# A second in-place fold in the bias network: eight key pairs to a packed tile, half the third-layer matmuls

## The chip, the cores and the metric

The kernel runs on one core of a Trainium2 chip. Its engines are TensorE (PE; its weight loads are shown as PEld), VectorE (DVE), ScalarE (ACT), GpSimd (POOL) and SyncE (SP); POOL and SP issue the DMAs of the stage that is changed here. The metric is the device time of one execution in microseconds. Three runs of the kernel before took 2696.52, 2698.0 and 2698.18 us, so their median is 2698.0 us.

## The reference

Four layers are computed one after the other on an image tensor; only the first matters here. It is a deformable attention block on x of shape (2, 512, 32, 32), with 8 heads of 64 channels. For every image and head, 64 key positions are found from the queries by an offset network, the input is sampled there, and keys and values are made from the samples. A small network of three layers gives a bias for every pair of one of the 1024 query pixels and one of the 64 keys:

```python
pos = grid_q[:, :, None, :] - grid_kv[:, None, :, :]
bias = jnp.sign(pos) * jnp.log1p(jnp.abs(pos))
bias = jax.nn.relu(bias @ cpb_w1 + cpb_b1)
bias = jax.nn.relu(bias @ cpb_w2 + cpb_b2)
bias = (bias @ cpb_w3 + cpb_b3).reshape(b, GROUPS, H * W, Hd * Wd)
sim = jnp.einsum('bhid,bhjd->bhij', qh, kh) + bias
attn = jax.nn.softmax(sim, axis=-1)
out = jnp.einsum('bhij,bhjd->bhid', attn, vh)
```

The hidden layers have 128 units. An output projection and an MLP follow in the same block, then the three other layers. All data is fp32.

## The kernel before

Two heads share a chunk of 128 channels, so there are 8 groups g (four chunks k, two images b) with 64 keys j, each key standing for both heads. One long loop goes through all 512 keys as 256 pairs p. A step number n counts keys; pair p covers n = 2p and 2p+1.

**First layer.** `first(n)` (L346, one custom VectorE instruction at L353) adds a table of column terms and one of row terms and clips at zero: a tile `h1` of 128 units by 2048 (pixels of both heads). Four such tiles exist (L343). The tables are loaded by SyncE (`tab_load`, L157) and scaled by ScalarE.

**Second layer.** `second(p, o)` (L612) runs for o = 0 to 3, each for 32 of the 128 hidden units. Eight matmuls (L619) write 32 output rows each, four of them side by side in the 128 rows of a `ph` tile (rows 32t to 32t+31 hold the quarter t of head and pixels), for the two keys of the pair. ScalarE applies bias and relu while copying to the tile `r0` to `r3` (L628); two `ph` tiles alternate.

**Third layer.** Its weights are not applied in one matmul over 128 units. Hidden units are ordered and scaled at the start of the kernel (`counted`, L462) so that units that are added unweighted share a weight's sign. `combine` (L631, VectorE, at L634) adds `r1` times a ratio to `r0`, and `r3` likewise to `r2`. `join` (L636, L637) adds `r2` to `r0` by an accumulating DMA from POOL's queue. `fold` (L639, L642) adds the odd rows of `r0` to the even rows, in place, by another one. `shift` (L644, a plain DMA by SyncE at L649) copies every fourth row of `r0` into a packed tile `xs`, and `meet` (L651, L653, POOL) adds the rows two further to them, so that a row of `xs` holds the sum of four neighbouring rows. Four pairs share an `xs` tile. `third` (L655, matmuls at L664) contracts packed tiles with the sparse weights `cw3` into `psim`: each call has four matmuls of 32 rows, and two calls accumulate into one `psim` tile, so that a group takes four calls, 16 matmuls.

**Order of the work.** Inside the loop all instructions of an engine keep the order in which the program issues them (`pin`). `at(n, when, fn)` puts work on a date; `run(n, when)` issues it at step n after an even o (when = 0) or an odd o (when = 1). Pair p is folded at step 2p+4, shifted at 2p+6 and met at 2p+7 (L909 to L911); the join of a pair is issued in the next pair after o = 1 (L942). Third-layer calls of a group stand at 64g + 16u + 24. `prepare` (L674) samples and projects keys and values of a group, from step 64(g-1) + 32 on; in it `keys` (L735, ScalarE) and `values` (L741, VectorE) copy into `kblk` and `vblk` in four pieces each. `weigh` (L747) and `weights` (L759) multiply values with the output weights into `vwo`, one slot for each of the 8 groups. `attend` (L780) does the softmax of a group, from step 64(g+1) + 9 on. `chain` (L913) computes the key positions of later groups; its 36 taps per call (L230, VectorE) are spread over steps 4 to 86 and 97 to 213. `r0` has five buffers, `xs` three.

After the loop the remaining folds, shifts and meets run, then the last third-layer call and the last softmax. Here the order is not pinned: the compiler's scheduler mixes in the output projection `po` (L1040, 64 matmuls, of which 32 belong to image 0). The `po` matmuls take `vwo` as weights. The MLP follows (L1105).

Of the kernel before, what the change touches and what calls it, by code (L numbers as in the profile page):

```python
# [10 lines left out]
F32 = mybir.dt.float32  # L11
AF = mybir.ActivationFunctionType
ALU = mybir.AluOpType
# [3 lines left out]
P = 128  # L17
B, C, H, W = 2, 512, 32, 32
# [39 lines left out]

_ORDER = [("same", P), ("below", P), ("place", P), ("rank", 1), ("third", 33)]
_CAT, _n = {}, 0  # L60
# [12 lines left out]
def conv_seq(  # L73
# [61 lines left out]
    with ExitStack() as ctx_l0:  # L135
# [11 lines left out]

        vwo = l0.tile([P, KC * B, C], F32, name="vwo")
        nc.gpsimd.memset(kblk, 0.0)
# [37 lines left out]
        def pin(ins):  # L187
            return tc.keep_in_program_order(ins) if started else ins
# [150 lines left out]
        sb3 = l0.tile([P, 4, 2], F32, name="sb3")  # L339
        cw3 = l0.tile([P, 33], F32, name="cw3")  # L340
        rel = l0.tile([P, 2], F32, name="rel")
# [23 lines left out]
        with tc.tile_pool(name="a", bufs=1) as a, tc.tile_pool(name="aps", bufs=3, space=PSUM) as aps, tc.tile_pool(  # L365
# [96 lines left out]
            def counted():  # L462
                pin(ve.tensor_copy(od[:, 7:9], pcnt))
                pin(ve.tensor_scalar(cpbw, cpbw, maj, None, ALU.mult))


                pin(ve.tensor_scalar(maj, total, 8.0, None, ALU.is_ge))
                pin(ve.tensor_scalar(t0, maj, -1.0, 1.0, ALU.mult, ALU.add))
                pin(ve.tensor_scalar(t1, total, -1.0, 16.0, ALU.mult, ALU.add))
# [125 lines left out]


        with tc.tile_pool(name="hid", bufs=3) as hid, tc.tile_pool(name="sm", bufs=1) as sm, tc.tile_pool(name="hps", bufs=2, space=PSUM) as hps, tc.tile_pool(
            name="sps", bufs=1, space=PSUM
# [13 lines left out]
            def second(p, o):  # L612

                ph = hps.tile([P, 2, 512], F32, name="ph")
                for i in range(2):
                    for t in range(4):
# [9 lines left out]
                        )  # L626
                r = hid.tile([P, 2, 512], F32, name=f"r{o}", bufs=(5, 1, 3, 1)[o])
                pin(nc.scalar.activation(r, ph, AF.Relu, bias=sb3[:, o, 1:2]))  # L628
# [9 lines left out]

            def fold(p):  # L639

                r = rs[p, 0]
                pin(nc.gpsimd.dma_start(r[0::2], r[1::2], accum_op=ALU.add))  # L642

            def shift(p):  # L644

                t, d = divmod(p, 4)
                if d == 0:
                    xs_[t] = hid.tile([P, 2, 512], F32, name="xs", bufs=3)
                pin(nc.sync.dma_start(xs_[t][d::4], rs[p, 0][0::4]))  # L649

            def meet(p):  # L651
                t, d = divmod(p, 4)
                pin(nc.gpsimd.dma_start(xs_[t][d::4], rs.pop((p, 0))[2::4], accum_op=ALU.add))  # L653

            def third(g, u):  # L655
                kb, i = divmod(u, 2)
                if i == 0:
                    psims[g, kb] = sps.tile([P, 512], F32, name=f"psim{kb}")
                for a in range(2):
                    xs = xs_.pop(g * J // 8 + 2 * u + a)  # L660
                    for c in range(2):
                        m = 2 * c + a
                        pin(
                            nc.tensor.matmul(  # L664
                                psims[g, kb][m * 32 : (m + 1) * 32, :],
                                lhsT=cw3[:, 1 - i : 33 - i],
                                rhs=xs[:, c, :],
                                start=(i == 0),
                                stop=(i == 1),
                                skip_group_check=True,  # L670
                            )
                        )

            def prepare(g):  # L674

                k, b = divmod(g, B)
                st = {}
                n = J * (g - 1) + 32
                here = slice(CO_AT[k] * P + b * J, CO_AT[k] * P + (b + 1) * J)
# [50 lines left out]
                def ordered(to, of):  # L730

                    to, of = to.rearrange("p (c x i) -> p c x i", c=2, i=2), of.rearrange("p (i x c) -> p c x i", c=2, i=2)
                    return to, of

                def keys():  # L735
                    for h, kb in np.ndindex(2, 2):
                        hs, ks = slice(h * DH, (h + 1) * DH), slice(kb * 32, (kb + 1) * 32)
                        to, of = ordered(kblk[hs, g % 2, h, ks], st["pk"][hs, 0, ks])
                        pin(nc.scalar.activation(to, of, AF.Identity, scale=DH**-0.5))

                def values():  # L741
                    for h, kb in np.ndindex(2, 2):
                        hs, ks = slice(h * DH, (h + 1) * DH), slice(kb * 32, (kb + 1) * 32)
                        to, of = ordered(vblk[hs, g % 2, h, ks], st["pk"][hs, 1, ks])
                        pin(nc.vector.tensor_copy(to, of))
# [13 lines left out]
                def weights():  # L759
                    pin(nc.scalar.copy(vwo[:, g, :], st["pw"]))  # L760

# [140 lines left out]
            for g in range(NG):  # L902
                prepare(g)
                for u in range(4):
                    at(J * g + 16 * u + 24, 0, third, g, u)
                if g < NG - 1:
                    attend(g, J * (g + 1) + 9, True)
            for p in range(NK // 2):
                at(2 * p + 4, 0, fold, p)  # L909
                at(2 * p + 6, 0, shift, p)  # L910
                at(2 * p + 7, 0, meet, p)  # L911

# [15 lines left out]

            chain(1, 2, 86, 82)
            chain(2, 4, 213, 116)  # L930

# [103 lines left out]
        for t in range(NT // 512):  # L1035
            ts_ = slice(t * 512, (t + 1) * 512)
            for o in range(KC):
                po = mh.tile([P, 512], F32, name="po")
                for k in range(KC):
                    nc.tensor.matmul(  # L1040
                        po,
                        lhsT=vwo[:, k * B + t // 2, o * P : (o + 1) * P],
                        rhs=q[:, k, ts_],
                        start=(k == 0),
                        stop=(k == KC - 1),
                    )
# [838 lines left out]
def _layout(a):  # L1885
# [50 lines left out]

    rank = p // 32 * 4 + p % 4
    same = p[:, None] % 32 // 4 == p[None] % 32 // 4
    put("same", same.astype(f), order)
    put("below", (same & (rank[:, None] < rank[None])).astype(f), order)  # L1940
    put("place", (np.array([0, 2, 1, 3])[p // 32] * 4 + p % 4).astype(f)[None], order)
    put("rank", rank.astype(f)[:, None], order)

    put("third", (np.arange(33)[None] == (1 + 8 * (p // 32) + 2 * (p % 4))[:, None]).astype(f), order)
    put("npy", -(4 * np.arange(8)[None] + p[:, None] // 32).astype(f))
# [56 lines left out]
```

## Time and profile before

| what | value |
|---|---|
| median of three runs | 2698.0 us |
| the profiled execution, own time | 2697.67 us |
| its span on the page | 2695.9 us, granted TensorE clock 0.996 |
| PE busy | 2653.6 us, 98% |
| VectorE busy | 2251.3 us, 84% |
| ScalarE busy | 1538.4 us, 57% |
| POOL busy | 669.8 us, 25% |
| second layer, L619 | 16384 matmul records, 1779.1 us |
| first layer, L353 | 512 instructions, 1172.9 us, 2291 ns each |
| `combine`, L634 | 512 instructions, 658.0 us, 1285 ns each |
| evictions, L628 | 1024 instructions, 1141.1 us, 1114 ns each |
| POOL's issues of join, fold, meet | 958, 857, 1198 ns each, 256 of each |

An fp32 matmul appears in the profile as two records. Busy shares are means over the whole program; the loop of the bias network fills 34 to 1901 us of it. An engine's idle time is listed with what ended it. For a DMA the page gives the time from its issue to its landing, and the issuing engine counts only the issue as busy.

### The profile page before, as it was taken

What the parts mean: (1) busy time and instruction counts of PE and PEld (TensorE: products, weight loads), DVE (VectorE), ACT (ScalarE), POOL (GpSimd) and SP (SyncE); (2) the same over time, 40 slices, a digit from 0 to 9 for tenths busy, and PEclk for the clock granted to TensorE, in tenths of its full rate; (3) what the DMA queues carried; (4) which work ended last, traced back from release to release, by engine and by line L of the source; (5) the groups of instructions that cost most, each with busy time, mean ns of one, the idle gap of its engine ahead of it and who ended that gap; (6) DMA issues with size and microseconds to landing.
All of it is one profiled execution on the core that took longest, in us unless ns stands there. A gap on an engine that the chain in (4) does not pass through costs nothing.

```text
span 2695.9 us, 48423 instructions
## 1 busy us (share of the span) xinstructions
PE 2653.6 (98%) x19574; PEld 967.3 (36%) x19574; DVE 2251.3 (84%) x2009; ACT 1538.4 (57%) x1920; POOL 669.8 (25%) x784
## 2 busy tenths in 40 slices
PE   8999999999999999999999999999999999999997
PEld 4223323232332323333333333333444444455544
DVE  6999999999999999999999999999554445525646
ACT  7676677777667777866877776776221111001334
POOL 0333333333333333333333333333100000000001
PEclk9999999999999999999999999999999999999998
DMA  4777877877777787787788788787400000100001
GB/s 129 165 165 162 168 158 161 169 157 162 163 166 158 165 170 157 165 168 161 162 195 173 154 179 188 163 174 159 94 30 24 16 24 24 62 17 1 1 0 63
DMA packets 109327, 335.04 MB, mean 124 GB/s; under 512 B 18576, under 2 KB 28304, under 8 KB 108336
## 3 DMA queue, kind: packets, MB, share of 16 engines
q0 software_dynamic: 69632, 234.93, 46.7%
q1 hardware_dynamic: 38896, 96.51, 10.4%
q8 instruction: 154, 2.52, 0.4%
q14 instruction: 69, 0.57, 0.1%
q10 hardware_dynamic: 576, 0.51, 0.1%
HBM read 58.99 MB, written 4.46 MB: 24 GB/s over the span
## 4 chain that ended last, share of the span: by engine, by line
PE 81%; DVE 9%; issue 6%; ACT 2%; DMA 1%; POOL 1%; DVEq 0%; ACTq 0%; POOLq 0%
PE ph L619 51%; DVE h L353 4%; PE A L1105 4%; PE D L1105 4%; PE C L1105 4%; DVE r L634 3%; PE B L1105 2%; PE po L1040 2%; PE pg L1248 1%; PE pa L1359 1%; PE pu L1282 1%; PE psim L664 1%; PE pscore L1491 1%; DMA xs<-r 1%; PE pt L1511 1%
## 5 line engine op out<-in xcount | busy, mean ns | idle before, releaser
L619 PE MATMUL ph<-h,w2a 128*32 128x512 f32 x16384 | 1779.1, 593 | 6.0 <-ACT r L628 3.3
L628 ACT ACTIVATE r<-ph,sb 128x1024 f32<-128x1024 f32 x1024 | 1141.1, 1114 | 510.5 <-PE ph L619 487.3
L353 DVE CUSTOM_DVE_ANT_1 h<-tab 128x2048 f32<-128x2048 f32 x512 | 1172.9, 2291 | 13.0 <-PE ph L619 10.0
L619 PEld LDWEIGHTS ph<-h,w2a 128*32 128x32 f32 x16384 | 520.2, 109 | 1226.6 <-issue 801.7
L634 DVE SCALAR_TENSOR_TENSOR r<-r,rel,r 128x1024 f32<-128x1024 f32 x512 | 658.0, 1285 | 16.4 <-ACT r L628 15.8
L642 POOL DMA_DIRECT2D r<-r x256 | 219.5, 857 | 961.2 <-DMA r<-r 936.1
L637 POOL DMA_DIRECT2D r<-r x256 | 245.2, 958 | 280.4 <-DVE r L634 243.6
L653 POOL DMA_DIRECT2D xs<-r x256 | 306.6, 1198 | 12.2 <-issue 6.1
L173 ACT ACTIVATE tab<-tab,vec 128x256 f32<-128x256 f32 x252 | 136.9, 543 | 0.0
L1293 POOL MEMSET M<- 128x512 f32 x2 | 1.0, 524 | 435.3 <-DVE x L1169 435.3
L1145 ACT COPY u<-A 128x512 f32<-128x512 f32 x16 | 9.4, 585 | 146.9 <-PE A L1105 146.9
L1776 POOL TENSOR_TENSOR x<-x,aff 128x512 f32<-128x512 f32 x7 | 7.0, 1031 | 329.0 <-ACT e L1741 329.0
L1124 ACT ACTIVATE h<-h,vec 128x512 f32<-128x512 f32 x32 | 23.1, 721 | 113.7 <-DVE h L1127 113.7
L1127 DVE TENSOR_TENSOR h<-C,u 128x512 f32<-128x512 f32 x32 | 22.1, 691 | 48.2 <-PE C L1105 47.9
L1105 PE MATMUL A<-xn,w 128*128 128x512 f32 x128 | 60.3, 593 | 0.8 <-DVE x L1047 0.8
L1105 PE MATMUL C<-hT,w 128*128 128x512 f32 x128 | 60.3, 592 | 0.0
L1105 PE MATMUL A<-h,w 128*128 128x512 f32 x128 | 60.1, 592 | 0.0
L1040 PE MATMUL po<-q,vwo 128*128 128x512 f32 x128 | 56.3, 594 | 0.0
L230 DVE SCALAR_TENSOR_TENSOR acc<-q,vec,acc 128x128 f32<-128x128 f32 (+3 forms) x88 | 46.2, 525 | 0.8
L1165 DVE TENSOR_TENSOR x<-D,x 128x512 f32<-128x512 f32 x32 | 22.1, 691 | 25.8 <-PE D L1105 25.7
L856 ACT ACTIVATE e<-e,den 128x64 f32<-128x64 f32 x128 | 41.8, 338 | 1.9 <-DVE den L852 1.9
L1165 DVE TENSOR_TENSOR x<-C,x 128x512 f32<-128x512 f32 x32 | 22.1, 690 | 24.8 <-PE C L1105 24.8
(365 smaller groups left out, 1867.6 us busy)
## 6 DMA issues: line engine op xcount, KB each, us to landing
r<-r POOLq DMA_DIRECT2D x256, 512.0 KB, 5.2
r<-r POOLq DMA_DIRECT2D x256, 256.0 KB, 3.4
xs<-r SPq DMA_DIRECT2D x256, 128.0 KB, 3.9
xs<-r POOLq DMA_DIRECT2D x256, 128.0 KB, 5.6
tab<-fd SPq DMA_DIRECT2D x63, 512.0 KB, 5.6
lw<-in_l_w_dram SPq DMA_DIRECT2D x5, 1024.0 KB, 9.0
x<-in_x_dram SPq DMA_DIRECT2D x4, 1024.0 KB, 10.5
w<-in_mlp_w_dram SPq DMA_DIRECT2D x8, 512.0 KB, 4.3
```

The lines of the kernel that those rows point to most:

```text
L173: return nc.scalar.activation(tf, tf if src is None else src[:, :, ax, :], AF.Identity, bias=0.0 if ax == 0 else v("L0_conv_cpb_b1"), scal ...
L230: pin(nc.vector.scalar_tensor_tensor(dst, src, wt_, dst, ALU.mult, ALU.add))
L353: nc.vector._custom_dve(TENSOR_ADD_SAT, out=h1, in0=columns.unsqueeze(1).to_broadcast([P, 32, 2, 32]), in1=rows_.unsqueeze(3).to_broadcast ...
L619: nc.tensor.matmul(ph[t * 32 : (t + 1) * 32, i, :], lhsT=w2a[:, o], rhs=h1s[2 * p + i][:, half * 16 : (half + 1) * 16, h, :], start=True, ...
L628: pin(nc.scalar.activation(r, ph, AF.Relu, bias=sb3[:, o, 1:2]))
L634: pin(nc.vector.scalar_tensor_tensor(r0, r1, rel[:, i : i + 1], r0, ALU.mult, ALU.add))
L637: pin(nc.gpsimd.dma_start(rs[p, 0], rs.pop((p, 2)), accum_op=ALU.add))
L642: pin(nc.gpsimd.dma_start(r[0::2], r[1::2], accum_op=ALU.add))
L653: pin(nc.gpsimd.dma_start(xs_[t][d::4], rs.pop((p, 0))[2::4], accum_op=ALU.add))
L1040: nc.tensor.matmul(po, lhsT=vwo[:, k * B + t // 2, o * P : (o + 1) * P], rhs=q[:, k, ts_], start=(k == 0), stop=(k == KC - 1),)
L1105: nc.tensor.matmul(banks[bank], lhsT=a[an][k], rhs=b_[bn_][k], start=(i < 4 and k == 0), stop=(k == n - 1), skip_group_check=True,)
L1165: nc.vector.tensor_tensor(to, t, to, ALU.add)
```

## The change

The packed sum is taken one step further by DMA. A second in-place fold adds rows that lie two apart (now sums of two) so that every fourth row of `r0` holds a sum of four; `shift` then copies every eighth row, and `meet` adds the rows four further. Eight pairs fill an `xs` tile, a row of it holds the sum of eight neighbouring rows, and a group takes two third-layer calls with four matmuls each, 8 in place of 16; nothing accumulates in `psim` between calls. The hidden units are ordered for classes of eight rows instead of four per quarter, `cw3` has 32 columns instead of 33, and the keys' order in `kblk` and `vblk` changes so that two copies do instead of four. `r0` gets a sixth buffer. `vwo` keeps only image 0; the weights of image 1 are written over `wo`, whose slice is not read any more. Some dates move by two steps.

```diff
-                r = hid.tile([P, 2, 512], F32, name=f"r{o}", bufs=(5, 1, 3, 1)[o])
+                r = hid.tile([P, 2, 512], F32, name=f"r{o}", bufs=(6, 1, 3, 1)[o])
...
-            def fold(p):
+            def fold(p, step):
                 r = rs[p, 0]
-                pin(nc.gpsimd.dma_start(r[0::2], r[1::2], accum_op=ALU.add))
+                pin(nc.gpsimd.dma_start(r[0 :: 2 * step], r[step :: 2 * step], accum_op=ALU.add))
             def shift(p):
-                t, d = divmod(p, 4)
+                t, d = divmod(p, 8)
                 if d == 0:
                     xs_[t] = hid.tile([P, 2, 512], F32, name="xs", bufs=3)
-                pin(nc.sync.dma_start(xs_[t][d::4], rs[p, 0][0::4]))
+                pin(nc.sync.dma_start(xs_[t][d::8], rs[p, 0][0::8]))
             def meet(p):
-                t, d = divmod(p, 4)
-                pin(nc.gpsimd.dma_start(xs_[t][d::4], rs.pop((p, 0))[2::4], accum_op=ALU.add))
-            def third(g, u):
-                kb, i = divmod(u, 2)
-                if i == 0:
-                    psims[g, kb] = sps.tile([P, 512], F32, name=f"psim{kb}")
+                t, d = divmod(p, 8)
+                pin(nc.gpsimd.dma_start(xs_[t][d::8], rs.pop((p, 0))[4::8], accum_op=ALU.add))
+            def third(g, kb):
+                psims[g, kb] = sps.tile([P, 512], F32, name=f"psim{kb}")
                 for a in range(2):
-                    xs = xs_.pop(g * J // 8 + 2 * u + a)
+                    xs = xs_.pop(g * J // 16 + 2 * kb + a)
...
-                                lhsT=cw3[:, 1 - i : 33 - i],
+                                lhsT=cw3,
                                 rhs=xs[:, c, :],
-                                start=(i == 0),
-                                stop=(i == 1),
+                                start=True,
+                                stop=True,
...
-                n = J * (g - 1) + 32
+                n = J * (g - 1) + 34
...
                 def values():
-                    for h, kb in np.ndindex(2, 2):
-                        hs, ks = slice(h * DH, (h + 1) * DH), slice(kb * 32, (kb + 1) * 32)
-                        to, of = ordered(vblk[hs, g % 2, h, ks], st["pk"][hs, 1, ks])
+                    for h in range(2):
+                        hs = slice(h * DH, (h + 1) * DH)
+                        to, of = ordered(vblk[hs, g % 2, h, :], st["pk"][hs, 1, :])
                         pin(nc.vector.tensor_copy(to, of))
...
-                    pin(nc.scalar.copy(vwo[:, g, :], st["pw"]))
+                    pin(nc.scalar.copy((vwo, wo)[b][:, k, :], st["pw"]))
...
-                for u in range(4):
-                    at(J * g + 16 * u + 24, 0, third, g, u)
+                for kb in range(2):
+                    at(J * g + 32 * kb + 42, 0, third, g, kb)
                 if g < NG - 1:
-                    attend(g, J * (g + 1) + 9, True)
+                    attend(g, J * (g + 1) + 11, True)
             for p in range(NK // 2):
-                at(2 * p + 4, 0, fold, p)
-                at(2 * p + 6, 0, shift, p)
-                at(2 * p + 7, 0, meet, p)
+                at(2 * p + 4, 0, fold, p, 1)
+                at(2 * p + 6, 0, fold, p, 2)
+                at(2 * p + 8, 0, shift, p)
+                at(2 * p + 9, 0, meet, p)
...
-            chain(1, 2, 86, 82)
-            chain(2, 4, 213, 116)
+            chain(1, 2, 88, 84)
+            chain(2, 4, 215, 116)
```

More of the change, by code (lines that the diff above doesn't have):

```diff
@@ L57 @@
 _CONSTS = [("ident", P), ("grid", 2 * J), ("gridf", J), ("npx", 1), ("npy", 8), ("sel3", 2)]
-_ORDER = [("same", P), ("below", P), ("place", P), ("rank", 1), ("third", 33)]
+_ORDER = [("same", P), ("below", P), ("place", P), ("rank", 1), ("third", 32)]
 _CAT, _n = {}, 0
@@ L146, in conv_seq @@
         smpp = ctx_att.enter_context(tc.tile_pool(name="smp", bufs=1))
-        vwo = l0.tile([P, KC * B, C], F32, name="vwo")
+        vwo = l0.tile([P, KC, C], F32, name="vwo")
         nc.gpsimd.memset(kblk, 0.0)
@@ L339, in conv_seq @@
         sb3 = l0.tile([P, 4, 2], F32, name="sb3")
-        cw3 = l0.tile([P, 33], F32, name="cw3")
+        cw3 = l0.tile([P, 32], F32, name="cw3")
         rel = l0.tile([P, 2], F32, name="rel")
@@ L464, in counted @@
                 pin(ve.tensor_scalar(cpbw, cpbw, maj, None, ALU.mult))
-                pin(ve.tensor_scalar(maj, total, 8.0, None, ALU.is_ge))
+                pin(ve.tensor_scalar(maj, total, 16.0, None, ALU.is_ge))
                 pin(ve.tensor_scalar(t0, maj, -1.0, 1.0, ALU.mult, ALU.add))
-                pin(ve.tensor_scalar(t1, total, -1.0, 16.0, ALU.mult, ALU.add))
+                pin(ve.tensor_scalar(t1, total, -1.0, 32.0, ALU.mult, ALU.add))
                 pin(ve.scalar_tensor_tensor(t0, t1, t0, below, ALU.mult, ALU.add))
@@ L730, in ordered @@
                 def ordered(to, of):
-                    to, of = to.rearrange("p (c x i) -> p c x i", c=2, i=2), of.rearrange("p (i x c) -> p c x i", c=2, i=2)
+                    to, of = to.rearrange("p (k c x) -> p k c x", k=2, c=2), of.rearrange("p (k x c) -> p k c x", k=2, c=2)
                     return to, of
                 def keys():
-                    for h, kb in np.ndindex(2, 2):
-                        hs, ks = slice(h * DH, (h + 1) * DH), slice(kb * 32, (kb + 1) * 32)
-                        to, of = ordered(kblk[hs, g % 2, h, ks], st["pk"][hs, 0, ks])
+                    for h in range(2):
+                        hs = slice(h * DH, (h + 1) * DH)
+                        to, of = ordered(kblk[hs, g % 2, h, :], st["pk"][hs, 0, :])
                         pin(nc.scalar.activation(to, of, AF.Identity, scale=DH**-0.5))
                 def values():
-                    for h, kb in np.ndindex(2, 2):
-                        hs, ks = slice(h * DH, (h + 1) * DH), slice(kb * 32, (kb + 1) * 32)
-                        to, of = ordered(vblk[hs, g % 2, h, ks], st["pk"][hs, 1, ks])
+                    for h in range(2):
+                        hs = slice(h * DH, (h + 1) * DH)
+                        to, of = ordered(vblk[hs, g % 2, h, :], st["pk"][hs, 1, :])
                         pin(nc.vector.tensor_copy(to, of))
@@ L1041, in conv_seq @@
                         po,
-                        lhsT=vwo[:, k * B + t // 2, o * P : (o + 1) * P],
+                        lhsT=(vwo, wo)[t // 2][:, k, o * P : (o + 1) * P],
                         rhs=q[:, k, ts_],
@@ L1934, in _layout @@
     put("sel3", (p[:, None] % 32 == np.array([1, 2])[None]).astype(f))
-    rank = p // 32 * 4 + p % 4
-    same = p[:, None] % 32 // 4 == p[None] % 32 // 4
+    rank = p // 32 * 8 + p % 8
+    same = p[:, None] % 32 // 8 == p[None] % 32 // 8
     put("same", same.astype(f), order)
     put("below", (same & (rank[:, None] < rank[None])).astype(f), order)
-    put("place", (np.array([0, 2, 1, 3])[p // 32] * 4 + p % 4).astype(f)[None], order)
+    put("place", (np.array([0, 2, 1, 3])[p // 32] * 8 + p % 8).astype(f)[None], order)
     put("rank", rank.astype(f)[:, None], order)
-    put("third", (np.arange(33)[None] == (1 + 8 * (p // 32) + 2 * (p % 4))[:, None]).astype(f), order)
+    put("third", (np.arange(32)[None] == (8 * (p // 32) + p % 8)[:, None]).astype(f), order)
     put("npy", -(4 * np.arange(8)[None] + p[:, None] // 32).astype(f))
```

## The prediction

> **What bounds the kernel now.** The bias network's loop runs from 34 to 1901 us. I cut it into windows first, then asked the waits of its two halves, then the timeline around one third-layer call, the groups, the DMA landings and the chain. Windows (columns: window, busy us and instruction count of PE, PEld, DVE, ACT, POOL, then clock, DMA share, GB/s):
>
> ```profile
> 400.00:600.00 200.00, 199.65 (x1863) 62.10 (x1859) 199.23 (x139) 145.20 (x171) 69.41 (x81) 1.00 0.79 163
> 1400.00:1600.00 200.00, 200.00 (x1854) 61.95 (x1846) 194.26 (x124) 146.48 (x178) 72.47 (x84) 1.00 0.80 169
> ```
>
> TensorE looks full in both, but a busy PE is modelled. VectorE tells them apart: 199.2 of 200 us early, 194.3 late. The waits of 100 to 860 us, then of 880 to 1850 us (us in total, times, longest):
>
> ```profile
> PEld ph L619 <- DVE h L353: 30.4, 45, 1.3
> DVE h L353 <- PE ph L619: 0.4, 1, 0.4
> ...
> DVE h L353 <- PE ph L619: 9.6, 8, 2.2
> DVE r L634 <- ACT r L628: 8.2, 15, 0.9
> ```
>
> Early, TensorE waits for VectorE's first layer (45 times) and VectorE for almost nothing: VectorE is the bound. Late, there is no line in which TensorE waits for VectorE, and VectorE waits for TensorE and for evictions of its results: TensorE is the bound. The turn comes near 876 us, key 228, where the 72 offset taps (L230) spread over the first 225 keys are through. First-layer starts 64 keys apart confirm it: 234.6 to 235.3 us up to key 256, 230.5 us from key 320 on.
>
> A third-layer call and POOL beside it, late in the loop (start, us, what):
>
> ```profile
> 953.81 0.13 PEld L664 LDWEIGHTS psim<-xs,cw 128*32 128x32 f32 x4 [0.30 <-issue]
> ...
> 954.24 0.13 PEld L664 LDWEIGHTS psim<-xs,cw 128*32 128x32 f32 x4 [0.30 <-issue]
> 954.26 0.86 POOL L642 DMA_DIRECT2D r<-r  x1 [3.14 <-DMA r<-r]
> ...
> 954.67 0.13 PEld L619 LDWEIGHTS ph<-h,w2a 128*32 128x32 f32 x4 [0.30 <-issue]
> ...
> 956.21 0.86 POOL L637 DMA_DIRECT2D r<-r  x1 [1.09 <-DVE r L634]
> 956.74 1.17 POOL L653 DMA_DIRECT2D xs<-r  x1
> ```
>
> Four third-layer matmuls (eight records, two per fp32 matmul) hold the queue from 953.81 to 954.67: 0.86 us, with no wait for `xs`. POOL's cycle is join, meet, wait for the join's landing, fold; here it waits 3.14 us for that landing.
>
> [...] in the timeline above sets of four records advance every 0.43 us, where one record lasts 0.59. [...] here POOL's issues stay at 0.86 us under a running L353, so I charge nothing.
>
> **The change, part by part.** *Third layer.* 16 matmuls per group become 8: two calls instead of four. Calls at keys 64g+16u+24 become 64g+32kb+42. In the TensorE-bound stretch (key 228 to 512) there are 18 calls before (keys 232 to 504) and 9 after (234 to 490); the last, (7,3) or (7,1), is in the tail on both sides. 9 x 0.86 = 7.7 us saved. The other calls, 13 before and 6 after, lie where VectorE is the bound: 6.0 us of TensorE time there gain nothing, since TensorE already idles for `h`. Does VectorE become the bound late? It needs 194.3/200 x 230.5 = 223.9 us a group; TensorE falls to 230.5 - 1.7 = 228.8. No.
>
> *Key order.* `keys` and `values` fall from four instructions to two of double width:
>
> ```profile
> L745 DVE COPY vblk<-pk 64x32 f32<-64x32 f32 x28 | 4.0, 183 | 5.5 <-ACT kblk L739 5.5
> ...
> L719 DVE COPY kv<-pkv 128x64 f32<-128x64 f32 x7 | 1.5, 219 | 0.0
> ```
>
> 4 x 0.183 - 2 x 0.219 = 0.29 us of VectorE per group. Groups 1 to 3 lie in the VectorE-bound stretch: 0.9 us gained; group 0 and the rest count zero, as does ACT (145 of 200 us busy).
>
> *The DMA chain.* Before, per pair: join 512, fold 256, shift 128, meet 128 KB. After: join 512, fold 256, second fold 128, shift 64, meet 64. The bytes are equal, 1024 KB. POOL gets a fourth issue. Landings before:
>
> ```profile
> r<-r POOLq DMA_DIRECT2D x256, 512.0 KB, 5.2
> r<-r POOLq DMA_DIRECT2D x256, 256.0 KB, 3.4
> xs<-r SPq DMA_DIRECT2D x256, 128.0 KB, 3.9
> xs<-r POOLq DMA_DIRECT2D x256, 128.0 KB, 5.6
> ```
>
> POOL's order becomes second fold (p-3), fold (p-2), join (p-1), meet (p-4). The second fold needs fold p-3, issued just before the previous join and landed 3.4 us later; its issue (0.86 us, the fold's row) fits into the wait for the join's landing, 509.5 us over 130 folds late in the loop, 3.9 us each. It would cost 0.86 us per pair if that wait were gone. Its 128 KB follow join and meet in the queue, and the next fold cannot start before the join lands. Shift still has one pair between it and its fold, meet one more; `r0` gets a sixth buffer for the added pair, and meet p-4 frees it for pair p+2, as meet p-3 did for p+2 with five. From a meet's issue to the eviction that reuses `r0` there are at least 8.6 us in the trace, typically 10.3, against the 5.6 landing; the third layer starts three keys after its last meet, as before. ACT waits for this landing 3.6 us in total now. I take +0.3 us for both reloads of `x`, which hold the ring for some 9 us; bounds 0 and +4.
>
> *Shifted dates* (prepare, attend, taps by two keys): no instruction more; two keys move from the slower to the faster rate, -0.2 to 0. I take 0. *Storage:* `vwo` halves and batch 1 reuses `wo`; its copy waits only for a matmul (L750) issued about a key earlier. 0.
>
> *Tail.* After the last second-layer matmul the data path is join, fold, second fold, shift, meet, third, one hop longer: fold landing 3.4 plus issue overlap, about +4 us. Chain and window before:
>
> ```profile
> 1901.77 16.57 PE po L1040 x38
> 1918.34 0.98 PE psim L664 x4
> ...
> 1931.77 30.06 PE po L1040 x70
> ```
>
> ```profile
> 1901.70:1962.00 60.30, 59.98 (x163) 27.19 (x162) 32.87 (x48) 7.15 (x24) 5.12 (x6) 1.00 0.26 64
> ```
>
> TensorE fills this path with output projections: 60.0 of 60.3 us. 19 of the 64 stand before the last third-layer half. In the changed program's TensorE order 27 do. 27 x 0.86 = 23.1 us after the start of projections; the last meet, issued at 1914.05, has landed by about 1917, 15 us after that start, so about 19 with the extra hop. Covered by 4 us; without the cover, +4. After it TensorE has ten projections to cover the softmax, before as well as after, and 26 instead of 35 remain after the last transpose, whose copy the next one waits for, perhaps 0.5 us. The weight loads wait for those transposes, so they come some 7 us later and still precede their use by over 10 us. Tail: 0, bounds -0.5 to +4.
>
> Sum against the profiled execution, 2697.67 us (span 2695.9, 1.8 around it): -7.7 - 0.9 + 0.3 = -8.3, so 2689.4. The median of the three runs is 2698.0, 0.3 higher: 2689.7.
>
> **Rivals.** (1) TensorE is the bound throughout: 16 calls leave the loop, 13.7 us, 2684. For it: PE reads 100% all along; against it: 45 waits for `h` early and VectorE's 199 of 200. (2) The tail shows the extra hop because its transfers land later than 23 us: +4, 2693.7. For it: one more accumulate in series; against it: 4 us of cover. (3) POOL's cycle becomes the bound, and it is slower than before. The second fold then stands in series with join and fold: in late pairs fold follows join by up to 6.5 us on a 16-pair mean, the next join 0.55 later, 7.05; with 0.86 more 7.9 us against a pair's 228.8/32 = 7.15. Over 142 late pairs 0.75 x 142 = 107, less some 10 of buffering: 2787. It decides where POOL's join-to-join time passes 7.15 us. Against it: the wait in which the issue fits. (4) The freed time turns into small waits for `r0` around the x reloads or elsewhere, half the gain: 2694.
>
> **How the numbers follow.** Forecast 0.62, rival 1 0.07, rival 2 0.14, rival 3 0.08, rival 4 0.09. About 0.2%, 5.4 us, is what a measurement here can tell from no change: faster means under 2692.6. Forecast and rival 1 are below; part of rival 2's spread (0.05) too: 0.74 faster. Same 0.18, slower 0.08. The range 2684.0 to 2696.0 holds rivals 1, 2 and 4 and leaves out rival 3.
>
> **What would show it.** L664 at 128 records instead of 256; late groups 228.8 us per 64 keys, early ones about 234.7; late VectorE still waiting for `ph`, never TensorE for `h`; POOL's first-fold wait near 3 us, no growth of ACT's wait for DMA; the last third-layer half without a wait, projections from start to end in about 60 us. The prediction is wrong if the late groups don't shorten by 1.7, if POOL's wait for the join's landing vanishes, or if TensorE idles ahead of the last third-layer matmuls.

## The result and the profile after

The changed kernel takes 2747.78 us in the median of five runs (2744.69 to 2748.65), where the kernel before takes 2697.85. The ratio is 1.0183, with a 95% interval of 1.0172 to 1.0195: 50 us slower, where 8 us faster was forecast. The profiled execution has a span of 2746.9 us against 2695.9, at a granted TensorE clock of 0.995 against 0.996. The two clocks differ by 0.1%, the two spans by 1.9%, so the clock is not the cause.

Where the 51.0 us of span lie, by the start times of the first layer: keys 4 to 260 take 946.5 us instead of 935.4 (+11.1), keys 260 to 508 take 929.2 instead of 892.0 (+37.2), and from the last first layer to the end it is 808.9 instead of 806.5 (+2.4). The few keys at both ends make up the rest. The same two windows as before the change (columns: window, then busy us and count of PE, PEld, DVE, ACT, POOL, clock, DMA share, GB/s):

```profile
400.00:600.00 200.00, 197.07 (x1823) 60.95 (x1819) 197.75 (x138) 144.08 (x173) 92.64 (x109) 1.00 0.84 160
1400.00:1600.00 200.00, 189.91 (x1750) 60.62 (x1746) 184.43 (x117) 131.09 (x147) 88.47 (x104) 1.00 0.85 167
```

In the late window TensorE stands at 189.9 of 200 us and VectorE at 184.4, so neither is the bound any more. The DMA engines are busier (0.85 against 0.80) and move no more bytes a second (167 GB/s against 169). The chain of work that ended last names the new bound, in its shares by engine:

```profile
DMA 52%; PE 34%; issue 5%; POOL 4%; DVE 3%; ACT 2%; DVEq 0%; POOLq 0%; ACTq 0%; SPq 0%
```

Before the change the shares were:

```profile
PE 81%; DVE 9%; issue 6%; ACT 2%; DMA 1%; POOL 1%; DVEq 0%; ACTq 0%; POOLq 0%
```

Half of that chain, 51%, was second-layer matmuls. The chain of after, followed in time, late in the loop (start, us, what), is one pattern over and over:

```profile
994.17 6.29 DMA r<-r
1000.46 0.29 issue
1000.75 0.46 POOL r L644
1001.21 0.08 issue
1001.29 6.13 DMA r<-r
1007.41 0.29 issue
1007.70 0.46 POOL r L644
```

A join's transfer runs for 6.1 to 6.3 us; 0.29 us after it has landed POOL issues the fold of the same pair; 0.54 us behind the fold goes the next pair's join, whose landing the next fold waits for. The chain comes back to its own start after 6.9 to 7.1 us here, so it is a closed ring: each join can be issued only when the join before it has landed. POOL's own timeline of the same stretch (L644 is both folds now, L639 join, L655 meet):

```profile
1000.75 0.85 POOL L644 DMA_DIRECT2D r<-r  x1 [2.77 <-DMA r<-r]
1001.29 1.22 POOL L639 DMA_DIRECT2D r<-r  x1
1001.86 1.46 POOL L655 DMA_DIRECT2D xs<-r  x1
1004.58 0.84 POOL L644 DMA_DIRECT2D r<-r  x1 [1.26 <-DMA r<-r]
1007.70 0.85 POOL L644 DMA_DIRECT2D r<-r  x1 [2.29 <-DMA r<-r]
```

The second fold (1004.58) does fit into the wait for the join's landing, as the prediction said, and POOL still waits 2.29 us after it. But the join has no wait for VectorE any more: it is issued straight behind the fold, 0.54 us after it in the median late in the loop. In the timeline of before it stood 1.95 us behind it, released by `combine`. The join now lags the end of its `combine` by 4.6 us in the median early in the loop (100 to 860 us) and 6.3 late; before it was 0.3 in both. The waits of the late stretch, 880 to 1850 us (us in total, times, longest):

```profile
POOL r L644 <- DMA r<-r: 510.8, 254, 4.9
PEld ph L621 <- ACT r L630: 248.2, 463, 3.2
...
ACT r L630 <- DMA r<-r: 36.9, 33, 2.7
ACT r L630 <- DMA xs<-r: 33.1, 16, 3.8
PE ph L621 <- ACT r L630: 31.8, 30, 2.3
...
POOL r L639 <- DVE r L636: 2.0, 2, 1.1
```

This is the path of the delay back to TensorE: buffers `r0` and `r2` come free late, ScalarE's evictions wait for these DMAs (70 us here and 40 us in the early stretch, against 3.6 and 1.2 us before), `ph` comes free late, and the matmuls wait. The last line is the sharpest: the join waits for VectorE in 2 pairs of this stretch. The first line holds the waits of both folds; those that a join's landing ended are 348.5 us over 130 folds, 2.7 us each. The landings of after (KB each, median us from issue):

```profile
r<-r POOLq DMA_DIRECT2D x256, 512.0 KB, 6.3
r<-r POOLq DMA_DIRECT2D x256, 256.0 KB, 3.5
r<-r POOLq DMA_DIRECT2D x256, 128.0 KB, 4.3
...
xs<-r SPq DMA_DIRECT2D x256, 64.0 KB, 3.3
xs<-r POOLq DMA_DIRECT2D x256, 64.0 KB, 6.2
```

The join moves the same 512 KB as before and lands after 6.3 us instead of 5.2. The meet moves half of what it did and takes longer, 6.2 instead of 5.6.

What the kernel before had of this could be read there. Its waits in the same stretch:

```profile
POOL r L642 <- DMA r<-r: 519.4, 133, 9.0
...
POOL r L637 <- DVE r L634: 75.4, 50, 4.1
...
ACT r L628 <- DMA xs<-r: 3.6, 6, 0.6
```

The first line is the wait that the prediction took as room (its figure is from a slightly shorter stretch). The second shows how much room there was: the join waited for VectorE in 50 of some 133 pairs, 75.4 us, that is 0.57 us a pair. The third is the ScalarE wait for DMAs that grew to 70 us.

### The profile page after: what moved, and what is told of

It reads as the page before. It is cut to its first block, busy times and chain, and to the rows that moved or that the text cites. A ratio compares the mean times of both kernels' runs of the same rounds, so it can differ in the third digit from the quotient of the medians.

```text
span 2746.9 us, 48171 instructions
## 1 busy us (share of the span) xinstructions
PE 2654.6 (97%) x19446; PEld 981.9 (36%) x19446; DVE 2254.7 (82%) x1993; ACT 1529.2 (56%) x1904; POOL 881.2 (32%) x1040
## 4 chain that ended last, share of the span: by engine, by line
DMA 52%; PE 34%; issue 5%; POOL 4%; DVE 3%; ACT 2%; DVEq 0%; POOLq 0%; ACTq 0%; SPq 0%
DMA r<-r 50%; PE ph L621 7%; PE A L1106 4%; PE D L1106 4%; PE C L1106 4%; POOL r L644 4%; PE B L1106 2%; DMA xs<-r 1%; PE pg L1249 1%; PE po L1041 1%; PE pa L1360 1%; PE pu L1283 1%; PE pscore L1492 1%; DVE h L354 1%; DVE r L636 1%
## 5 line engine op out<-in xcount | busy, mean ns | idle before, releaser
L621 PEld LDWEIGHTS ph<-h,w2a 128*32 128x32 f32 x16384 | 538.1, 109 | 1266.8 <-issue 749.2
L644 POOL DMA_DIRECT2D r<-r x512 | 431.8, 844 | 1028.4 <-DMA r<-r 999.8
L655 POOL DMA_DIRECT2D xs<-r x256 | 364.6, 1424 | 6.1 <-DMA xs<-r 3.5
L639 POOL DMA_DIRECT2D r<-r x256 | 309.6, 1210 | 66.5 <-DVE r L636 63.8
L1249 PE MATMUL pg<-xt 128*128 128x512 f32 (+3 forms) x128 | 36.4, 439 | 1.4 <-ACT xt L1247 1.1
## 6 DMA issues: line engine op xcount, KB each, us to landing
x<-in_x_dram SPq DMA_DIRECT2D x4, 1024.0 KB, 12.3
```

The costliest lines, as they stand in the source:

```text
L621: nc.tensor.matmul(ph[t * 32 : (t + 1) * 32, i, :], lhsT=w2a[:, o], rhs=h1s[2 * p + i][:, half * 16 : (half + 1) * 16, h, :], start=True, ...
L639: pin(nc.gpsimd.dma_start(rs[p, 0], rs.pop((p, 2)), accum_op=ALU.add))
L644: pin(nc.gpsimd.dma_start(r[0 :: 2 * step], r[step :: 2 * step], accum_op=ALU.add))
L655: pin(nc.gpsimd.dma_start(xs_[t][d::8], rs.pop((p, 0))[4::8], accum_op=ALU.add))
L1249: nc.tensor.matmul(pgs[i], lhsT=xt[:, i * P : (i + 1) * P], rhs=xt[:, i * P :], start=(t == 0), stop=(t == 7),)
```

## The experiments

There were three theories at first: (1) the ring of join, landing, fold and next join, which POOL's order of issue closes; (2) the packing by every eighth row, slow in itself; (3) the throughput of the DMA engines, which might be used up at a share of 0.85. Periods and landings below that no shown line has are worked out from the issue and landing times of the traces, late stretch (880 to 1840 us) unless said.

**Taking the ring apart by dates.** `later_folds` is the changed kernel with each fold, shift and meet one pair later, so that a join has a whole pair more to land before its fold is due; a seventh `r0` buffer, and the dates that depend on it, follow.

```diff
-                at(2 * p + 4, 0, fold, p, 1)
-                at(2 * p + 6, 0, fold, p, 2)
-                at(2 * p + 8, 0, shift, p)
-                at(2 * p + 9, 0, meet, p)
+                at(2 * p + 6, 0, fold, p, 1)
+                at(2 * p + 8, 0, fold, p, 2)
+                at(2 * p + 10, 0, shift, p)
+                at(2 * p + 11, 0, meet, p)
...
```

> The changed kernel with both folds, shift and meet of a pair one pair later (2p+6, 2p+8, 2p+10, 2p+11), a seventh r0 buffer, and third, attend, prepare and taps two steps later. Same transfers, same bytes, same matmuls. Theory 1 (POOL's order is the recurrence: a fold waits for the landing of the join issued just before, and the next join stands behind that fold): the wait for the join's landing vanishes, the pair time returns to the engines, about 2690 us (2687 to 2696). Theory 2 (the new packing, 16-row transfers every eighth row, is slow in itself): no change, about 2745. Theory 3 (the DMA engines have no throughput left at a share of 0.84): no change either, 2740 or more.

Measured: 2689.77 us, ratio 0.9972 [0.9963, 0.9982]. It is faster than both kernels, 8 us or 0.3% below the kernel before, and at the time forecast for the change. Its waits late in the loop, and its two windows:

```profile
POOL r L639 <- DVE r L636: 346.1, 117, 5.9
...
POOL r L644 <- DMA r<-r: 97.3, 66, 6.2
```

```profile
400.00:600.00 200.00, 198.47 (x1843) 61.65 (x1839) 199.30 (x140) 146.84 (x175) 92.78 (x108) 1.00 0.85 162
1400.00:1600.00 200.00, 200.00 (x1850) 62.13 (x1846) 195.66 (x122) 147.18 (x177) 96.67 (x114) 1.00 0.89 176
```

POOL waits for VectorE again, TensorE is full late, and the DMA engines carry a share of 0.89 without being the bound. Theory 3 falls, theory 2 in its pure form too: all transfers are the same as in the changed kernel. The ring is confirmed. A seventh buffer without the later dates was not tried. But in the changed kernel the join's inputs were ready 4.6 to 6.3 us before it was issued, so a buffer that came free late is not what held it.

`before_later` gives the kernel before the same later fold, shift and meet, with six `r0` buffers and the smaller `vwo`.

```diff
-                at(2 * p + 4, 0, fold, p)
-                at(2 * p + 6, 0, shift, p)
-                at(2 * p + 7, 0, meet, p)
+                at(2 * p + 6, 0, fold, p)
+                at(2 * p + 8, 0, shift, p)
+                at(2 * p + 9, 0, meet, p)
...
```

> The kernel before with its fold, shift and meet one pair later, a sixth r0 buffer and the dates and the storage of vwo of the changed kernel; third layer and packing as before. Theory 1: POOL's cycle was not the bound before, so about the same, 2695 to 2699 us, and POOL's wait for the join's landing falls from 3.9 us per late pair to nearly 0. If it was already costing time in late pairs, 2690 to 2695.

Measured: 2698.52 us, 1.0007 [0.9998, 1.0015]. The later dates, the buffer and the storage are worth nothing by themselves at full work; the kernel before was not bound by its ring.

**Is it the second fold?** `no_fold2` is the changed kernel without it, so that half of the terms of the bias are left out; `thin_fold2` keeps its issue and its 32 rows but only 64 columns of one key, and leaves out the rest of the addition.

```diff
-                at(2 * p + 6, 0, fold, p, 2)
```

> The changed kernel without the second fold (left out: sums of eight rows become sums of two rows each, so half of the terms are missing from the bias). Everything else stays: dates, buffers, packing by eight, eight third-layer matmuls. Theory 1: about 2689 us (2685 to 2695), since the fourth issue and its transfer leave POOL's cycle. Theory 2 (packing): about 2745. Theory 3 (throughput): in between, 2690 to 2720, since 128 of 960 KB of POOL's transfers are gone.

```diff
-                pin(nc.gpsimd.dma_start(r[0 :: 2 * step], r[step :: 2 * step], accum_op=ALU.add))
+                to, of = r[0 :: 2 * step], r[step :: 2 * step]
+                if step == 2:
+                    to, of = to[:, 0, 0:64], of[:, 0, 0:64]
+                pin(nc.gpsimd.dma_start(to, of, accum_op=ALU.add))
```

> The changed kernel with the second fold kept as an issue with its waits and its completion, but on 64 columns of one key only (32 rows of 256 bytes instead of 4 KB; left out: most of the second addition). If it is the 128 KB in the queue that lengthens the join's landing, about 2690 to 2697 us; if it is the issue, its place in POOL's order or its completion, 2735 to 2750.

Measured: `no_fold2` 2708.97 us, 1.0046 [1.0031, 1.0061]; `thin_fold2` 2836.93 us, 1.0520 [1.0504, 1.0535]. Both miss what was expected. Without the second fold 39 us come back, but the kernel is still slower than the one before, and late in the loop its joins still lag `combine` by 4.6 us. With the second fold thinned to 256 bytes a row the kernel is 89 us slower than with the whole one. Its median pair is 7.23 us and the mean 7.90, so it is some pairs that become very long; why, stays open. So this run doesn't price the issue alone, as it was meant to.

**The ring's own price.** Something besides the second fold lengthens the ring. Four kernels leave out half of the second layer and the combines, so that the engines need far less time than the ring and only the ring can set the period:

```diff
                 for o in range(4):
                     n = 2 * p + o // 2
-                    second(p, o)
+                    if o % 2 == 0:
+                        second(p, o)
                     if o == 1 and p:
-                        combine(p - 1, 2)
                         join(p - 1)
-                    elif o == 3:
-                        combine(p, 0)
...
-            combine(NK // 2 - 1, 2)
```

> The kernel before with half of the second layer left out (the hidden units of r1 and r3, and with them both combines), so that TensorE needs about 3.5 us a pair and VectorE about 4.6: POOL's ring of join, landing and fold is then the only thing that can set the pair period, and the period is its price. Theory A (something in the changed kernel besides the second fold, the packing by every eighth row or the buffers and dates, lengthens the ring): a period as in the 66 back-to-back pairs of the kernel before, 6.3 to 6.8 us, so a time near 2698 - 1867 + 256 x 6.6 = 2520. Theory B (any sustained back-to-back ring is slower than a short burst of it, whatever the packing): 7.0 to 7.4 us, near 2670.

> The ring of the kernel before, with the changed kernel's buffers and dates: shift and meet one pair later, six r0 buffers, the smaller vwo; packing by every fourth row as before, half of the second layer left out. Theory A splits here: near the ring of the kernel before if the packing by every eighth row is what lengthens the ring, near the ring without the second fold if buffers and dates are. Theory B: equal to both.

> The changed kernel without its second fold (half the terms of the bias are missing) and with the same half of the second layer left out. Theory A: a period of 7.0 to 7.3 us as in the kernel without the second fold at full work, near 2660, some 130 us above the ring of the kernel before. Theory B: the same period as the ring of the kernel before, within 0.1 us or 25 us of time.

> The changed kernel with the same half of the second layer left out. Both theories: the second fold's own price in the ring is 0.15 us a pair, as between the changed kernel (7.50 us) and the one without the second fold (7.33), so some 40 us above the ring without it. If the ring falls by more than 0.3 us against 7.5, the cycle at full work was also lengthened by the engines' other work.

| ring of | time, us | pair, median / mean, us | from a fold's landing to the landing of the join behind it, median, us |
|---|---|---|---|
| the kernel before | 2580.29 | 6.32 / 6.91 | 2.76 |
| before, with the new dates and buffers | 2596.44 | 6.32 / 6.98 | 2.75 |
| the changed kernel without second fold | 2672.46 | 6.97 / 7.27 | 3.39 |
| the changed kernel | 2721.09 | 7.16 / 7.41 | 3.27 |

Theory A holds: the old ring sustains 6.32 us in the median when nothing else holds it (its time was expected 60 us lower, with a mean pair of 6.6 us where 6.9 was measured). In these rings dates and buffers cost 16 us, the packing 76 us, the second fold 49 us. The granted clock is 0.91 to 0.92 in all four, so it doesn't separate them. And `ring_after`, with half of the second layer gone, is only 27 us faster than the changed kernel at full work: the ring sets nearly all of its time. Landings in the ring of before and in the ring without the second fold:

```profile
r<-r POOLq DMA_DIRECT2D x256, 512.0 KB, 5.5
r<-r POOLq DMA_DIRECT2D x256, 256.0 KB, 3.3
xs<-r SPq DMA_DIRECT2D x256, 128.0 KB, 3.7
xs<-r POOLq DMA_DIRECT2D x256, 128.0 KB, 5.5
```

```profile
r<-r POOLq DMA_DIRECT2D x256, 512.0 KB, 6.1
r<-r POOLq DMA_DIRECT2D x256, 256.0 KB, 3.3
...
xs<-r SPq DMA_DIRECT2D x256, 64.0 KB, 3.8
xs<-r POOLq DMA_DIRECT2D x256, 64.0 KB, 5.9
```

With 128 KB less to move per pair, the fold lands as before and the join 0.6 us later. The single packets show where. The durations in us of the last 16 packets of 4 KB of a join, in one typical pair of each ring (some 16 are under way at a time):

```
ring of before:      0.34 0.34 0.34 0.34 0.34 0.34 0.33 0.34 0.34 0.35 0.34 0.34 0.34 0.34 0.34 0.35
without second fold: 0.54 0.38 0.48 0.36 0.47 0.64 0.67 0.36 0.55 0.55 0.67 0.72 0.35 0.82 0.34 0.92
```

Up to there the packets of the fold and the join take 0.34 to 0.37 on average in both. These pairs are typical: over the 131 and 129 late pairs whose packets can be told apart from those of other pairs, 0.9% and 54% of a join's last 16 packets take over 0.42 us, and of its other packets 0.3% and 1.3%. The shift's packets, or others from SyncE, are not the cause: of the last 16 without a packet of another queue beside them, 0.8% and 45% are slow. In the changed kernel at full work 11% of the 4 KB packets of POOL's queue take over 0.42 us, in the kernel before 2%. Of the meet's packets, behind the join's, it is 20% and 0.9% (late pairs in which POOL's queue moves its 240 or 224 packets of 4 KB in one stretch, counted in the order of their starts).

**What in the packing.** `ring_meet16` is the ring with the new dates, old packing, and a meet of only 16 of its 32 rows.

```diff
-                pin(nc.gpsimd.dma_start(xs_[t][d::4], rs.pop((p, 0))[2::4], accum_op=ALU.add))
+                pin(nc.gpsimd.dma_start(xs_[t][d::8], rs.pop((p, 0))[2::8], accum_op=ALU.add))
```

> The ring of the kernel before with the changed kernel's buffers and dates (6.32 us in the median, 2596 us; packing by every fourth row, half of the second layer left out), with the meet adding only half of its 32 rows, 16 rows eight apart, and the shift unchanged at 32 rows (so half of the meet's terms are left out too). If the meet's 16 packets are what slows the join's last round: 6.9 to 7.0 us, 2670. If it is the shift's 16 rows: 6.2 to 6.35 us, 2560 to 2600.

Measured: 2669.67 us against 2596.44, pair 6.76 in the median, 7.28 in the mean. Halving the meet alone costs 73 us, although fewer bytes are moved. The shift still moves 32 rows there. In time, that is all but 3 us of what the packing costs; in the median pair it is 0.44 of 0.65 us. The next five vary the ring without the second fold (2672.46) in the place or the layout of the meet's rows (only their times count: except in `ring_halves` the meet's rows go to other places, come from other places or are left out of the bias):

`ring_rows`, neighbouring rows in the destination, and in that of the shift too:

```diff
-                pin(nc.gpsimd.dma_start(xs_[t][d::8], rs.pop((p, 0))[4::8], accum_op=ALU.add))
+                pin(nc.gpsimd.dma_start(xs_[t][16 * d : 16 * d + 16], rs.pop((p, 0))[4::8], accum_op=ALU.add))
```

> The ring without the second fold (half of the second layer and the second fold left out, 6.97 us in the median, 2672 us), with the 16 rows that a pair gives to shift and meet written to 16 neighbouring rows of the packed tile instead of to every eighth (the third layer's weights are not adapted, so the sums are mixed up). In that ring the join's last round of 4 KB packets and the meet's 16 packets took 0.4 to 1.1 us each, against 0.34 in the ring of the kernel before. If rows eight apart in the destination get in each other's way: 6.3 to 6.5 us, 2560 to 2600 us. If it is [...] the rows of the source: unchanged, 2672.

`ring_source`, neighbouring rows in the source:

```diff
-                pin(nc.gpsimd.dma_start(xs_[t][d::8], rs.pop((p, 0))[4::8], accum_op=ALU.add))
+                pin(nc.gpsimd.dma_start(xs_[t][d::8], rs.pop((p, 0))[64:80], accum_op=ALU.add))
```

> The same ring, with the meet reading 16 neighbouring rows of r0 instead of every eighth (the wrong rows, only their place counts) and writing to every eighth row as in the changed kernel. If rows eight apart in the source get in each other's way: 6.3 to 6.5 us, 2560 to 2600 us. If it is the destination, or the count of packets: unchanged, 2672. Both of these rings fast would say that either side has to be eight apart on both to conflict.

`ring_halves`, two stretches of 2 KB for each of the meet's 16 rows, and of the shift's (the third layer, shift and meet use columns 0 to 511 of the padded tile):

```diff
-                    xs_[t] = hid.tile([P, 2, 512], F32, name="xs", bufs=3)
+                    xs_[t] = hid.tile([P, 2, 520], F32, name="xs", bufs=3)
...
```

> The ring without the second fold (6.97 us, 2672 us), with the rows of the packed tile padded between the two keys, so that the meet's and the shift's 16 rows go as 32 packets of 2 KB, [...] instead of 16 of 4 KB. [...] If it is the 16 places in the destination: 6.9 to 7.1 us, 2660 to 2690.

`ring_step7`, rows seven apart in a spare tile that nothing reads:

```diff
-                pin(nc.gpsimd.dma_start(xs_[t][d::8], rs.pop((p, 0))[4::8], accum_op=ALU.add))
+                pin(nc.gpsimd.dma_start(spares[p % 2][d : d + 106 : 7], rs.pop((p, 0))[4::8], accum_op=ALU.add))
```

> The ring without the second fold (6.97 us in the median, 2672 us), with the meet's 16 rows added into a spare tile that nobody reads, at rows seven apart (half of the second layer, the second fold and the meet's terms left out). [...] 6.3 to 6.6 us, 2570 to 2620. If it is only that there are 16 rows: unchanged, 2660 to 2690.

`ring_step4`, rows four apart in one half of the spare tile:

```diff
-                pin(nc.gpsimd.dma_start(xs_[t][d::8], rs.pop((p, 0))[4::8], accum_op=ALU.add))
+                pin(nc.gpsimd.dma_start(spares[p % 2][64 * (d // 4) + d % 4 : 64 * (d // 4) + 64 : 4], rs.pop((p, 0))[4::8], accum_op=ALU.add))
```

> The control for it: the same spare tile, with the 16 rows four apart in one half of the partitions. [...] If the spare tile itself is what helps: as with rows seven apart.

Measured: `ring_rows` 2725.46, `ring_source` 2672.80, `ring_halves` 2672.18, `ring_step7` 2674.73, `ring_step4` 2663.16 us. Neighbouring rows make it worse by 53 us; the shift's were moved with the meet's, so the meet's own part is not separated. Nothing makes it better by more than 10: not the source's rows, not rows in two stretches of 2 KB, and not another spacing in the destination, where rows four, eight and seven apart lie within 12 us. So the step from rows four apart to rows eight apart is not what separates 16 rows from 32. What is shown is that a ring whose meet moves 16 rows takes 2663 to 2725 us in every place tried, against 2596.44 with 32 (`ring_before_dates`), and that the join ahead of the meet then lands later: 3.17 us behind the fold in `ring_meet16` and 3.39 in `ring_no_fold2`, against 2.75. Rows and bytes were halved together, and which of the two counts was not separated. Why the packets take longer stays open.

**At full work.** Three kernels test this on the changed kernel with its own dates. (Rows seven apart have no time at full work: beside the two spare tiles of `step7_after`, 0.875 KB of on-chip memory a partition was left for tiles that need 4.125 KB.) `rows_after` has the neighbouring rows of `ring_rows`, with the third layer's weights set to match:

```diff
-    put("third", (np.arange(32)[None] == (8 * (p // 32) + p % 8)[:, None]).astype(f), order)
+    put("third", (np.arange(32)[None] == (8 * (p % 16 // 4) + p // 16)[:, None]).astype(f), order)
...
```

> The changed kernel at full work and with its own dates, but a pair's 16 sums in 16 neighbouring rows of the packed tile, with the third layer's weights set to match. If the destination's spacing is what slowed the ring, its cycle falls by about 0.6 us, from 7.16 to some 6.55 us in the median, under the 7.15 us that a pair needs: 2690 to 2700 us. If not: 2748 as before.

`halves_after`, the padded tile of `ring_halves`:

> The changed kernel at full work and with its own dates, with the same padded rows. If the count of packets is the cause, the ring falls by some 0.6 us under the 7.15 us that a pair needs: 2690 to 2700 us. If it is the places: 2740 to 2760.

`wide_meet`, whose meet moves 32 rows again, beside the second fold (into a spare tile that nothing reads, so the meet's terms are left out):

```diff
-                pin(nc.gpsimd.dma_start(xs_[t][d::8], rs.pop((p, 0))[4::8], accum_op=ALU.add))
+                pin(nc.gpsimd.dma_start(spare[d % 4 :: 4], rs.pop((p, 0))[2::4], accum_op=ALU.add))
```

> The changed kernel at full work, with its own dates and its second fold, but its meet moves 32 rows four apart as before the change (128 KB instead of 64, into a spare tile that nobody reads, so the meet's terms are left out of the bias). [...] rows seven apart and four apart gave the same ring as eight apart. If a meet of 16 rows, whatever its places, is what takes the ring past the 7.15 us that a pair needs: the ring falls from 7.16 to some 6.5 to 6.7 us in the median and the time to 2690 to 2710, although 64 KB more are moved per pair. If bytes or the second fold decide: 2745 to 2765.

Measured, in this order: 2776.02 us (1.0283 [1.0249, 1.0317]), 2752.39 (1.0203 [1.0185, 1.0221]) and 2712.28 (1.0064 [1.0047, 1.0080]). Neither neighbouring rows nor stretches of 2 KB help. `wide_meet` moves 64 KB more per pair than the changed kernel and is 35 us faster, a little slower than expected. Its landings:

```profile
r<-r POOLq DMA_DIRECT2D x256, 512.0 KB, 5.9
...
spare<-r POOLq DMA_DIRECT2D x256, 128.0 KB, 6.2
```

Its early pairs (7.34 us in the median, 7.31 in the mean) are as long as those of the kernel before (7.31), where VectorE is the bound; late a pair still takes 7.35 in the mean, and 19% of the whole chain is DMA `r<-r`, so the ring still binds in part. Of the 58 us between the changed kernel and `later_folds`, undoing the meet's 16 rows returns 35, undoing the second fold 39. The two overlap, since either one brings a late pair close to the engines' own 7.15 us (7.35 in the mean in `wide_meet`, 7.33 in `no_fold2`).

**TensorE's account.** `later_third2` is `later_folds` with every third-layer matmul issued twice.

```diff
                     for c in range(2):
                         m = 2 * c + a
-                        pin(
+                        for _ in range(2):
+                            pin(
```

> The changed kernel with later dates (2689.8 us) with every third-layer matmul issued twice, so that TensorE has the 16 matmuls a group of the kernel before. The forecast's account, TensorE the bound only from key 228 on: 9 calls of 0.86 us, +7.7, so 2697.5. TensorE the bound throughout: 15 calls, +13, 2702.7. TensorE no bound at all: 2690.

Measured: 2702.04 us, 12.3 above `later_folds` in the medians and 10.8 in the two profiled executions, nearer to "bound throughout" than to the forecast's account. The first layer's pitch tells how: late groups go from 228.8 to 230.6 us, the 1.8 that two calls of 0.86 give; early ones (the second to the fourth) from 234.0 to 234.2 to between 234.9 and 235.8. So adding calls costs something early too: keys 4 to 260 take 936.7 us instead of 932.6, 4.1 for seven calls of 0.86. But taking them out of the kernel before gained only 0.2 to 1.2 us per early group (234.4 to 235.2 became 234.0 to 234.2): VectorE and TensorE are nearly tied there. That the tie counts one way, so that more TensorE work costs and less gains little, is the likely reading, and not shown by itself.

## Why the prediction was wrong

**The step that failed** is the DMA chain: "its issue (0.86 us, the fold's row) fits into the wait for the join's landing, 509.5 us over 130 folds late in the loop, 3.9 us each", and with it the charge of +0.3 us. The issue does fit: POOL still waits 2.29 us behind it in the timeline of after. But that wait was not room. It is a link of a closed ring: the next join stands behind the fold in POOL's order, so when a landing comes later, everything comes later. The prediction wrote down that "the next fold cannot start before the join lands", and did not close the circle. The ring of before takes 6.32 us in the median and 6.91 in the mean (`ring_before`) of the 7.15 to 7.23 that a late pair has, so the room was about 0.3 us in the mean. Signs of how small it was stood in the figures of before: the join's waits for VectorE were 0.57 us a pair, and rival 3's own sum, 7.05 against 7.15 us, left 0.1. The changed ring takes 7.16 and 7.41 with nothing beside it, and 7.51 in the mean at full work. Some 0.3 us a pair, over the 124 pairs of keys 260 to 508, are the 37 us. Early in the loop, where a pair of the kernel before takes 7.31 us, the same ring costs the other 11.

**The term that was mis-sized** is the join's landing. Both it and the meet were priced by bytes ("The bytes are equal, 1024 KB"). The join went from 5.2 to 6.3 us. Straight behind the fold it takes 5.5 in the ring of before already. In the rings 0.65 us of the median pair came with the packing, 0.44 of it from the meet of 16 rows alone (in time, nearly all of it), and 0.19 with the second fold.

**Rival 3** was the right mechanism, with its turning point of 7.15 us, and had 0.08. Its price was wrong: 0.86 us for an issue in series gave 7.9 us a pair and 2787. It is the slower landing and not the issue, and 7.51 us a pair in the mean.

**Third layer.** Right: with the ring out of the way late groups take 228.8 us (`later_folds`), the forecast figure, and keys 260 to 508, with eight calls fewer (6.9 us by 0.86 each), go from 892.0 to 885.3 us. The early stretch, keys 4 to 260, gains 2.8 us, of which 1.8 was forecast: 0.9 for `keys` and `values`, and 0.9 for one call fewer after key 228. The whole comes to 2689.77 where 2689.7 was forecast for the change. That they agree so closely is in part luck: the early stretch gained 1.0 us more than forecast, and the tail took 1.0 us longer.

**Shifted dates, storage.** Right at zero at full work (`before_later`). **Tail.** Forecast 0 with bounds of -0.5 and +4; from the last first layer to the end it is +1.0 us in `later_folds` and +2.4 in the changed kernel, whose backlog the chain carries into the last third-layer half at 1975.12. So the extra hop shows only in small part, and rival 2's +4 us is not what decided the result.

**Signs.** L664 has its 128 records. "No growth of ACT's wait for DMA" was the good sign: late it grew from 3.6 to 70 us. "If POOL's wait for the join's landing vanishes" was a bad one: the wait stayed, at 2.7 us a fold, and does not vanish in a ring that waits for itself. The sign to name was POOL's wait for VectorE ahead of the join, 75.4 us before and 2.0 after.

## What to carry to other kernels

An issuing engine's idle time is room only if what ends it comes from elsewhere: here 3.9 us of it a fold held some 0.3 us of room. Where the engine waits for its own transfer and issues the next one after that, it is a ring: set the ring's sum against the period that the other engines need, and look at how long the next issue still waits for its producer. Give each step of such a chain a whole period between a transfer and its use: with one more buffer and later dates the same change gained 8 us instead of losing 50. Price a DMA by its shape and by what stands ahead of it and behind it in the queue, and not by bytes alone: here a meet of half the bytes landed after 6.2 us instead of 5.6, and the join ahead of it, with the same bytes, after 6.3 instead of 5.2.

## What was not expected of the hardware

Halving an accumulating DMA (one that adds to what stands at its destination) from 32 rows of 4 KB to 16 rows made the DMA ahead of it in POOL's queue land 0.4 to 0.6 us later (2.75 to 3.17 us behind the fold in `ring_meet16`, 3.39 in `ring_no_fold2`): of the join's last 16 packets of 4 KB, which took 0.34 us each, 54% took over 0.42 in `ring_no_fold2`, up to 0.92 in the pair shown. The destination's rows seven, four or eight apart gave 2663 to 2675 us, neighbouring ones, with the shift's, 2725. An accumulating DMA of 32 rows of 256 bytes in place of 4 KB made the kernel 89 us slower. And a DMA share of 0.89 of the 16 engines, over the 200 us from 1400 us on in `later_folds`, was no bound.
